# Handing rows to the experts through a table of token numbers, and a rearranged opening, in a two-layer transformer block

## The chip, the cores and the metric

The kernel runs on one core of one Trainium2 chip, in float32 throughout. The metric is the device time of one run in microseconds (us). All data start and end in DRAM (HBM).

## The reference, cut to what matters

The input is `[8, 256, 512]`: 2048 tokens of 512 channels. Two layers follow each other. Each normalises its input and adds attention and a feed-forward network to it, side by side:

```python
xn = layernorm(x)
x  = x + linear_attention(xn)    # 32 heads of 128, decayed in blocks of 32; rms norm, sigmoid gate, output weights
       + experts(xn)
xn = layernorm(x)
x  = x + attention(xn)           # one head of 128, softmax, with biases
       + low_rank_ffn(xn)        # 64 pairs of rank 16, the best 16 of each token

def experts(xt):
    scores = softmax(xt @ router_w + router_b) + router_bias        # 16 experts
    g      = scores in 4 groups of 4; keep the 2 groups with the best maximum
    idx    = the best 2 experts in the groups kept;  gate = their scores, 0 elsewhere
    y      = sum over the experts e of gate[:, e] * ((silu(xt@w1[e]+b1[e]) * (xt@w2[e]+b2[e])) @ w3[e] + b3[e])
    z      = (silu(xt@sw1+sb1) * (xt@sw2+sb2)) @ sw3 + sb3          # shared expert, 256 wide
    return y + z
```

So each token uses two of sixteen experts. `b3` (in the kernel an array of 17 rows) holds the sixteen last biases `b3[e]` and, as row 16, the shared expert's `sb3`.

## The kernel before, in words

**Four chunks.** The tokens are cut into four chunks of 512 (`i` = 0 to 3), each with four tiles of 128 rows.

**The opening** runs the chunks one after the other. `begin` normalises a chunk (`normalize`: statistics, L231 and L232; a square root on ScalarE, L223; scaling, L236) and writes it into `xns[i]`. TensorE turns it, channels onto partitions (`turn_rows`, L243), and VectorE and ScalarE copy it to `xT[i]` (L246, L248). GpSimd makes sums of `xT` that the big products need later (`token_sums`, stored to `xc`). `shared_up` projects the chunk to the shared expert's width (wide products of 512 columns, L312). `route` computes the sixteen router scores by narrow products of 16 columns (L271), and a chain on VectorE ranks them (`first_two`: each score is compared with every other) into the gates `ge` and the choice `sel_all`. `decays` makes the attention's decay tables (stored to `dec`), and `clear` writes zeros from SBUF over a quarter of `xd`, an array in DRAM of 47 tiles of 128 rows. One chunk later `share` calls `shared_down`: it turns the gates (L333), copies them to `geT` (L335), and sums in one bank the product of gates and last biases (L338) and those of the shared expert (L340). The sum is added to `x` (L97 through the helper `tt`) and stored to `xr`.

**The slots.** When all chunks are routed, three products count the tokens of each expert (L482 to L484) and a chain on VectorE gives every pair of token and expert a slot. The slots of one expert begin on a tile of 128, so each of the 47 tiles of slots has one expert. The working tiles of this computation lie in `disp`, which takes the memory of the later accumulator `acc` (pool accp). The tiles of the routing (`sel_all`, `ge`, `before`) lie in the opening's pool, whose memory the next pool, `attn`, takes over; its first tiles `c` are written at L1010 and L1012.

**Attention, 32 units.** A unit is a chunk and a group of four heads; it needs the projections q, k, gate and v for its tokens. These are a large matrix product, made as a scheme of seven block products, `p1` to `p7`, each with weights `w` and tokens `xt` that are sums of blocks (`product`, L666). `ORDER` is the order in which their weights are made. In the first chunk (i = 0) the weights' sums are made on the way: VectorE adds blocks of a loaded tile `st` (`outer_sum`), GpSimd makes further sums, and they are stored to `ws` for the other chunks. For i = 1 to 3 each of the seven is again made by seven products (`p1` ... `p7` of `Outer`). After every group of four products `slot()` is called: it runs the pieces of other work that `later(n, f)` has entered for n slots ahead. The attention's scores, the output product (`project`, L858, whose operands `gT` GpSimd adds), and the experts come in that way. VectorE adds the results (`c`, `r`), GpSimd as well.

**Rows to the experts.** During i = 0 two rows tiles per unit are loaded from `xnd` (`row`), and each is written twice into `xd` by a DMA with computed addresses (`scatter`), 256 KB each, at its tokens' slots:

```python
out=xd[:, :],
out_offset=bass.IndirectOffsetOnAxis(ap=slots[:, n, t : t + 1], axis=0), in_=x_,
```

**Experts.** From unit 8 on, two or three slot tiles are worked per unit, 47 in all. `Expert` loads its tile of `xd` on SP's queue (L696) and gathers its expert's weights from GpSimd (L697). At slot 8 `turn` turns the rows, at 11 `up` computes the hidden values, at 14 `down` multiplies by the last weights, ScalarE copies the result to `ye` (L733) and it goes to `yd`. These tiles come from a ring of two staging buffers (`staged`), which `st`, `spare` and others share.

**Ends of the chunks.** In the last unit of a chunk, `load_sum` loads `xr[i]` into a staging buffer (`spare8`), and `finish` (L592) adds the attention to it; the result goes to `xs_[i]`. For the last chunk this is done in layer 1 (`next_x`). `gather` and `settle` fetch a token's two expert rows from `yd` and add them with their gates. For chunk 0 this stands in the last units (`wrapped_up`), followed by the normalisation for layer 1.

**Layer 1** goes chunk by chunk: `Head` makes the router's narrow products (`route`, 64 columns, L1316), q and k (`qk`, L1310), values, softmax and gates; `low_rank` and the last product use the scheme of seven again (L1434, L1512).

**Who orders the work.** The order in the program text is the order on each engine, save where the tile framework's scheduler moves instructions; in the pool `attn` ScalarE and GpSimd keep the program's order (`manual_schedule`). SP issues the plain DMAs; GpSimd issues those with computed addresses, between its other instructions.

Of the kernel before, what the change touches and what calls it, by code (L numbers as in the profile page):

```python
# [9 lines left out]
FP = mybir.dt.float32  # L10
I32 = mybir.dt.int32
# [55 lines left out]
def block_kernel(  # L67
# [75 lines left out]
    def once(shape, name):  # L143
        return work.tile(shape, FP, tag=name, name=name, bufs=1)

    scratch = big("scratch").rearrange("p (h b) n -> p h (b n)", h=4)
    xs = [work.tile([P, TPC, C], FP, tag="x", name=f"x{i}", bufs=NCH) for i in range(NCH)]
    x_t = x.rearrange("(i t p) c -> i t p c", t=TPC, p=P)
    for t in range(TPC):
        nc.sync.dma_start(out=xs[0][:, t, :], in_=x_t[0, t])  # L150
# [14 lines left out]
    b3_t = held[0 : E + 1, SH * C : (SH + 1) * C]  # L165
    nc.sync.dma_start(out=b3_t, in_=b3)
# [8 lines left out]
    xd = dram.tile([NSLOT, C], FP, name="xd")  # L175
# [7 lines left out]
    xnd = [dram.tile([P, TPC, C], FP, name=f"xnd{i}") for i in range(NCH)]  # L183
# [5 lines left out]
    zero = held[:, (SH + 1) * C : (SH + 2) * C].unsqueeze(1)  # L189
    nc.gpsimd.memset(zero, 0.0)  # L190

    ident = const.tile([P, P], FP, name="ident")
    make_identity(nc, ident)
    eps_t = const.tile([P, 1], FP, name="eps_t")
    nc.gpsimd.memset(eps_t, EPS)
# [5 lines left out]
    before = once([P, E, E], "before")  # L201
# [8 lines left out]
    dist = const.tile([P, S + P], FP, name="dist")  # L210
# [15 lines left out]
    def normalize(o, xc):  # L226

        mv = small.tile([P, TPC, 2], FP, tag="mv", name="mv")
        for t in range(TPC):
            st = small.tile([P, 6], FP, tag="st", name="st")  # L230
            nc.vector.bn_stats(st, xc[:, t, :])  # L231
            nc.vector.bn_aggr(mv[:, t, :], st)  # L232
        rstd = small.tile([P, TPC], FP, tag="rstd", name="rstd")
        rsqrt(rstd, mv[:, :, 1])
        for t in range(TPC):
            nc.vector.tensor_scalar(  # L236
                o[:, t, :], xc[:, t, :], mv[:, t, 0:1], rstd[:, t : t + 1], ALU.subtract, ALU.mult
            )
# [26 lines left out]
    def route(xT, ge, sel):  # L265

        full = [P, TPC, E]
        pl = ps_sc()
        for t in range(TPC):
            for c in range(NC):  # L270
                mm(  # L271
                    pl[:, bass.ts(t, E)], xT[:, c, bass.ts(t, P)], rw[:, c, :],
                    start=(c == 0), stop=(c == NC - 1),
                )
# [31 lines left out]
        tt(ge[:, :, 0:E], sc, sel, ALU.mult)  # L306
        nc.vector.memset(ge[:, :, E : E + 1], 1.0)
# [9 lines left out]
    def shared_up(i):  # L317
        hT = scratch[:, 2 + i % 2, :].rearrange("p (e n) -> p e n", e=SH)
        for e in range(SH):
            p1, p2 = ps_mm(), ps_mm()  # L320
            project(p1, wsh, e, i)
            project(p2, wsh, SH + e, i)
            h1 = work.tile([P, CH], FP, tag="h1", name="h1")
            b1, b2 = bsh_t[:, 0, e : e + 1], bsh_t[:, 1, e : e + 1]
            nc.scalar.activation(h1, p1, AF.Silu, bias=b1)
            nc.vector.scalar_tensor_tensor(hT[:, e, :], p2, b2, h1, ALU.add, ALU.mult)
        return hT

    def shared_down(i, hT):
        xc = xs[i]  # L330
        pg = ps_sc()
        for t in range(TPC):
            nc.tensor.transpose(pg[0 : E + 1, bass.ts(t, P)], gates[i][:, t, :], ident)  # L333
        gT = work.tile([E + 1, CH], FP, tag="geT", name="geT", bufs=1)
        nc.scalar.copy(gT, pg[0 : E + 1, :])  # L335
        for t in range(TPC):
            py = ps_mm()
            mm(py, gT[:, bass.ts(t, P)], b3_t, start=True, stop=False)  # L338
            for e in range(SH):
                mm(py, hT[:, e, bass.ts(t, P)], w3sh[:, e, :], start=False, stop=(e == SH - 1))  # L340
# [4 lines left out]
    sel_all = once([P, NTT, E], "sel_all")  # L345

    def share(i, hT):
        shared_down(i, hT)
        nc.sync.dma_start(out=xr[i], in_=xs[i])
# [60 lines left out]
    def clear(i):  # L410
        lo, hi = (0, 12, 24, 36, NMT)[i : i + 2]
        nc.sync.dma_start(
            out=xd[lo * P : hi * P, :].rearrange("(j p) c -> p j c", p=P),
            in_=zero.to_broadcast([P, hi - lo, C]),
        )

    def begin(i):
        xns.append(work.tile([P, TPC, C], FP, tag="xn", name=f"xn{i}"))
        normalize(xns[i], xs[i])
# [3 lines left out]
    for i in range(NCH):  # L423
# [3 lines left out]
        nc.sync.dma_start(out=xnd[i], in_=xns[i])  # L427
# [8 lines left out]
        ups.append(shared_up(i))  # L436
        ge = once([P, TPC, E + 1], f"ge{i}")
        route(xT[i], ge, sel_all[:, bass.ts(i, TPC), :])
        gates.append(ge)
        decays(i)  # L440
        clear(i)
# [8 lines left out]
    disp = Parts(accp.tile([P, 7 * CH], FP, tag="acc", name="disp"))  # L450
# [50 lines left out]
    nc.vector.tensor_reduce(own, owner, AX.X, ALU.add)  # L501
    nc.vector.tensor_scalar(own, own, float(E - 1), float(P), ALU.min, ALU.mult)
# [14 lines left out]
    for n in range(TOP):  # L517
        tt(hit, slot, ends_[:, n, :].unsqueeze(2).to_broadcast(full), ALU.is_equal)
        tt(hit, hit, sel_all, ALU.mult)
        for i in range(NCH):  # L520
            at_i = bass.ts(i, TPC)
            tt(hit[:, at_i, :], hit[:, at_i, :], gates[i][:, :, 0:E], ALU.mult)
# [63 lines left out]
    def finish(i, r):  # L586

        for b in range(2):
            for t in range(2):
# [4 lines left out]
                )  # L594

# [3 lines left out]
    with tc.tile_pool(name="attn", bufs=1) as attn, tc.manual_schedule(engines={mybir.EngineType.Activation, mybir.EngineType.Pool}):  # L599
# [79 lines left out]
        def slot():  # L679
# [3 lines left out]
            while pieces and pieces[0][0] <= now[0] and n < (2 if len(pieces) > 12 else 1):  # L683
                f = pieces.pop(0)[2]
                f()
                n += getattr(f, "func", f).__name__ not in ("silu", "gate", "row", "scatter", "load_sum", "sums1", "sums2", "sums3", "sums4", "settle0", "settle1", "out_sum")


        class Expert:


            def __init__(self, j):
# [3 lines left out]
                nc.sync.dma_start(out=self.xe, in_=xd[bass.ts(j, P), :])  # L696
# [6 lines left out]
            def turn(self):  # L703
# [4 lines left out]
                nc.vector.tensor_copy(self.xeT, pt.rearrange("p (c n) -> p c n", c=NC))  # L708

# [16 lines left out]
            def down(self):  # L726
# [6 lines left out]
                nc.scalar.copy(ye, py)  # L733
# [888 lines left out]
```

## Time and profile before

| | |
|---|---|
| runs of the kernel before | 2862.28, 2861.57, 2854.19 us; median 2861.57 |
| the profiled execution | 2856.16 us, of which the span in the trace is 2854.4 |
| TensorE products (PE) / weight loads (PEld) | busy 2796.7 / 2566.1 us (98% / 90% of the span) |
| VectorE (DVE), ScalarE (ACT), GpSimd (POOL) | busy 1569.7, 948.2, 1465.7 us (55%, 33%, 51%) |
| DMA | 763.21 MB, mean 267 GB/s |
| granted clock of TensorE | 0.993 |

| stage | from, to (us) | PE busy | 
|---|---|---|
| opening, to the third weight tile (p6) of the first unit | 0 to 186.7 | 160.65 |
| the rest of the first chunk, i = 0 | 186.7 to 764 | 570.31 |
| chunks 1 to 3, with the experts | 764 to 2535 | 1756.48 |
| layer 1 | 2535 to 2854 | 309.22 |

Busy times of the engines overlap, so they don't add up to the span. The stages' limits are read from the timeline, where a stage's first product of TensorE starts. In rows of the trace a tile's name stands for all its buffers, `a<-b` means that `a` is written from `b`, and L with a number is the line of the kernel (L97 is the helper that makes additions, so such rows are told apart by their tiles). A number in brackets at the end of a timeline row is the wait ahead of that group and what ended it.

### The profile page before, as it was taken

What the parts mean: (1) busy time and instruction counts of PE and PEld (TensorE: products, weight loads), DVE (VectorE), ACT (ScalarE), POOL (GpSimd) and SP (SyncE); (2) the same over time, 40 slices, a digit from 0 to 9 for tenths busy, and PEclk for the clock granted to TensorE, in tenths of its full rate; (3) what the DMA queues carried; (4) which work ended last, traced back from release to release, by engine and by line L of the source; (5) the groups of instructions that cost most, each with busy time, mean ns of one, the idle gap of its engine ahead of it and who ended that gap; (6) DMA issues with size and microseconds to landing.
All of it is one profiled execution on the core that took longest, in us unless ns stands there. A gap on an engine that the chain in (4) does not pass through costs nothing. (4 is left out here: it accounts for less than half of the span.)

```text
span 2854.4 us, 49572 instructions
## 1 busy us (share of the span) xinstructions
PE 2796.7 (98%) x19864; PEld 2566.1 (90%) x19864; DVE 1569.7 (55%) x2615; ACT 948.2 (33%) x1683; POOL 1465.7 (51%) x1213
## 2 busy tenths in 40 slices
PE   8989999999999999999999999999999999999999
PEld 4469999999999999999999999999999999987877
DVE  6555666666654445444545555555555555556663
ACT  3312222212244333333443333443444333432221
POOL 4545666665546555555645454545544566552210
PEclk9999999999999999999999999999999999999999
DMA  7888998899986777778877777777777788652211
GB/s 255 301 309 337 357 352 341 341 349 347 364 320 246 262 266 273 282 270 299 296 265 257 264 266 265 259 274 280 284 259 259 267 310 298 222 212 88 76 61 61
DMA packets 161943, 763.21 MB, mean 267 GB/s; under 512 B 18209, under 2 KB 24225, under 8 KB 109874
## 3 DMA queue, kind: packets, MB, share of 16 engines
q1 hardware_dynamic: 149826, 706.25, 66.9%
q0 software_dynamic: 11888, 53.79, 5.2%
q8 instruction: 157, 2.57, 0.4%
q14 instruction: 72, 0.59, 0.1%
HBM read 596.14 MB, written 163.05 MB: 266 GB/s over the span
## 5 line engine op out<-in xcount | busy, mean ns | idle before, releaser
L666 PE MATMUL ps_a<-xt,w 128*128 128x128 f32 x5376 | 750.9, 276 | 11.7 <-DVE r L97 7.7
L666 PEld LDWEIGHTS ps_a<-xt,w 128*128 128x128 f32 x5376 | 681.9, 192 | 30.1 <-issue 14.3
L97 POOL TENSOR_TENSOR c<-c 128x512 f32<-128x512 f32 x216 | 271.7, 1273 | 262.0 <-DVE c L97 259.9
L97 POOL TENSOR_TENSOR c<-c,r 128x512 f32<-128x512 f32 x240 | 318.4, 1347 | 158.9 <-DVE r L97 153.1
L666 PE MATMUL ps_e<-xt,w 128*128 128x128 f32 x2688 | 373.4, 275 | 1.3 <-DVE c L97 1.3
L97 POOL TENSOR_TENSOR sums<-sums,sq 128x512 f32<-128x512 f32 x120 | 153.3, 1278 | 426.4 <-ACT sq L796 425.6
L996 ACT COPY cp<-ps_a 128x512 f32<-128x512 f32 x336 | 196.4, 585 | 476.0 <-PE ps_a L666 468.8
L666 PEld LDWEIGHTS ps_e<-xt,w 128*128 128x128 f32 x2688 | 344.4, 192 | 11.2 <-issue 3.8
L97 POOL TENSOR_TENSOR w<-w 128x512 f32<-128x512 f32 x224 | 294.6, 1325 | 108.2 <-issue 31.2
L666 PE MATMUL ps_a<-w,xt 128*128 128x128 f32 x1792 | 346.7, 275 | 0.0
L858 PE MATMUL ps_sc<-wo,gT 128*128 128x256 f32 x1288 | 305.1, 379 | 1.8 <-POOL gT L97 1.8
L97 DVE TENSOR_TENSOR acc<-ps_sc,acc 128x512 f32<-128x512 f32 x208 | 143.3, 690 | 265.8 <-PE ps_sc L858 198.8
L666 PEld LDWEIGHTS ps_a<-w,xt 128*128 128x128 f32 x1792 | 272.3, 192 | 0.0
L97 DVE TENSOR_TENSOR c<-ps_a,c 128x512 f32<-128x512 f32 x232 | 157.9, 686 | 202.7 <-PE ps_a L666 201.7
L858 PEld LDWEIGHTS ps_sc<-wo,gT 128*128 128x128 f32 x1288 | 232.3, 190 | 26.8 <-POOL gT L97 2.0
L666 PE MATMUL ps_b<-xt,w 128*128 128x128 f32 x1680 | 236.4, 277 | 6.8 <-ACT c L1010 4.2
L801 DVE SCALAR_TENSOR_TENSOR gT<-ps_o,nw,c 128x256 f32<-128x256 f32 x256 | 112.0, 479 | 231.0 <-ACT sq L796 222.0
L666 PEld LDWEIGHTS ps_b<-xt,w 128*128 128x128 f32 x1680 | 217.3, 194 | 17.5 <-issue 8.2
L744 ACT ACTIVATE c<-c 128x512 f32<-128x512 f32 x256 | 148.9, 627 | 170.1 <-DVE c L97 170.0
L796 ACT ACTIVATE sq<-ps_o 128x512 f32<-128x512 f32 x120 | 71.6, 597 | 382.3 <-PE ps_o L782 382.3
L666 PE MATMUL ps_e<-w,xt 128*128 128x128 f32 x896 | 173.2, 275 | 0.0
L97 DVE TENSOR_TENSOR s<-ps_sc,decay 128x384 f32<-128x384 f32 x256 | 139.8, 552 | 40.7 <-PE ps_sc L770 38.1
(299 smaller groups left out, 4635.8 us busy)
## 6 DMA issues: line engine op xcount, KB each, us to landing
w<-in_w_att_dram SPq DMA_DIRECT2D x128, 1024.0 KB
st<-in_w_att_dram SPq DMA_DIRECT2D x32, 1024.0 KB
wo<-in_w_out_dram SPq DMA_DIRECT2D x113, 256.0 KB
decay<-dec SPq DMA_DIRECT2D x64, 384.0 KB
w<-ws0p SPq DMA_DIRECT2D x12, 1792.0 KB
w<-ws1p SPq DMA_DIRECT2D x12, 1792.0 KB
w<-ws2p SPq DMA_DIRECT2D x12, 1792.0 KB
w<-ws3p SPq DMA_DIRECT2D x12, 1792.0 KB
```

What stands on the lines that cost most here:

```text
L97: (eng or nc.vector).tensor_tensor(o, a, b, op)
L666: mm(bank[:, bass.ts(ty, P)], a, b, start=(first and ty == 0), stop=True, skip_group_check=True,)
L744: nc.scalar.activation(qk, qk, AF.Silu)
L796: nc.scalar.activation(sq, po, AF.Square)
L801: nc.vector.scalar_tensor_tensor(gT[:, h, :].rearrange("p (t n) -> p t n", t=2), po[:, bass.ts(h, S)].rearrange("p (t n) -> p t n", t=2), ...
L858: mm(py[:, bass.ts(t, S)], self.O[p][:, hh, bass.ts(t, P)], self.wo[p][:, hh, :], start=(t == 0 and hh == 0), stop=(hh == 1), skip_group_c ...
L996: nc.scalar.copy(c, bank)
```

## The change

The text of the computation is the same; what moves is this.

1. **A table in place of copied rows.** `xd`, its clearing and the loading of rows are gone. An array `table` of one integer per slot is zeroed once; in i = 0 each `scatter` writes 128 token numbers (from `token`, an iota) into it. At the end of i = 0 `read_table` loads the table and `turn_table` turns it by one transpose into `whose`, a tile of 128 x 47 integers. An expert then gathers its rows from `xnd` (now one array of 2048 rows) through `whose`, on GpSimd's queue.
2. **Last biases.** `shared_down` has no gates and no products with `b3`. Each `Expert` gathers its expert's bias into the buffer of its rows once they are turned (`bias`, through `own_`), and VectorE adds it in place of ScalarE's copy to `ye`. `sb3` is added to the rows of `xr` by GpSimd, at `load_sum` or `next_x` (`last_bias`). The slots of an expert's pieces move from 8, 11, 14 to 10, 12, 13, 18.
3. **Opening.** x of chunk 0 comes on two queues and is normalised tile by tile (`apart`); ScalarE's first square root is on a constant. Sixteen transposes of the identity stand at the beginning (`idle`). The router's narrow products stand among the wide ones (`between` in `shared_up`), the next chunk is turned ahead of `share`. `sel_all`, `before` and `ge` lie in `disp`, whose tile is taken first.
4. **Layer 1.** The normalisation in `wrapped_up` is spread over slots; the router products of the first `Head` stand among those of q and k (`opening`).

```diff
+WARM = 8
...
+    disp = Parts(accp.tile([P, 7 * CH], FP, tag="acc", name="disp"))
...
-        nc.sync.dma_start(out=xs[0][:, t, :], in_=x_t[0, t])
+        (nc.scalar if t % 2 else nc.sync).dma_start(out=xs[0][:, t, :], in_=x_t[0, t])
...
-    b3_t = held[0 : E + 1, SH * C : (SH + 1) * C]
-    nc.sync.dma_start(out=b3_t, in_=b3)
...
-    zero = held[:, (SH + 1) * C : (SH + 2) * C].unsqueeze(1)
-    nc.gpsimd.memset(zero, 0.0)
-
+    table = dram.tile([NSLOT, 1], I32, name="table")
+    none = once([NMT, P], "none", I32)
+    nc.gpsimd.memset(none, 0)
+    nc.sync.dma_start(out=table.rearrange("(j p) o -> j (p o)", p=P), in_=none)
+
+    eps_t = const.tile([P, 1], FP, name="eps_t")
+    nc.vector.memset(eps_t, EPS)
+    root = small.tile([P, TPC], FP, tag="rstd", name="root")
+    nc.scalar.activation(root[:, 0:1], eps_t, AF.Sqrt)
...
+    for _ in range(2):
+        idle = ps_o()
+        for n in range(WARM):
+            nc.tensor.transpose(idle[:, bass.ts(n % 4, P)], ident, ident)
...
-    before = once([P, E, E], "before")
+    before = disp.tile([P, E, E], FP, name="before")
...
-        tt(ge[:, :, 0:E], sc, sel, ALU.mult)
-        nc.vector.memset(ge[:, :, E : E + 1], 1.0)
+        tt(ge, sc, sel, ALU.mult)
...
-    def shared_up(i):
+    def shared_up(i, between):
...
             project(p1, wsh, e, i)
+            between()
             project(p2, wsh, SH + e, i)
+            between()
...
-        pg = ps_sc()
-        for t in range(TPC):
-            nc.tensor.transpose(pg[0 : E + 1, bass.ts(t, P)], gates[i][:, t, :], ident)
-        gT = work.tile([E + 1, CH], FP, tag="geT", name="geT", bufs=1)
-        nc.scalar.copy(gT, pg[0 : E + 1, :])
         for t in range(TPC):
             py = ps_mm()
-            mm(py, gT[:, bass.ts(t, P)], b3_t, start=True, stop=False)
             for e in range(SH):
-                mm(py, hT[:, e, bass.ts(t, P)], w3sh[:, e, :], start=False, stop=(e == SH - 1))
+                mm(py, hT[:, e, bass.ts(t, P)], w3sh[:, e, :], start=(e == 0), stop=(e == SH - 1))
...
-        normalize(xns[i], xs[i])
+        normalize(xns[i], xs[i], apart=(i == 0))
...
-        ups.append(shared_up(i))
-        ge = once([P, TPC, E + 1], f"ge{i}")
-        route(xT[i], ge, sel_all[:, bass.ts(i, TPC), :])
+        pl, tiles = ps_sc(), list(range(TPC))
+        ups.append(shared_up(i, lambda: scores(pl, xT[i], tiles.pop(0))))
+        ge = disp.tile([P, TPC, E], FP, name=f"ge{i}")
+        route(pl, ge, sel_all[:, bass.ts(i, TPC), :])
         gates.append(ge)
+        if i + 1 < NCH:
+            turn(i + 1)
         decays(i)
-        clear(i)
...
+    nc.vector.tensor_scalar(own_, own, float(E - 1), None, ALU.min)
...
+    def last_bias(r, t3):
+
+        nc.sync.dma_start(out=t3, in_=b3[E : E + 1].to_broadcast([P, C]))
+        for t in range(TPC):
+            add(r[:, t, :], r[:, t, :], t3, nc.gpsimd)
...
-                nc.sync.dma_start(out=self.xe, in_=xd[bass.ts(j, P), :])
+                nc.gpsimd.indirect_dma_start(
+                    out=self.xe, out_offset=None, in_=xnd[:, :],
+                    in_offset=bass.IndirectOffsetOnAxis(ap=whose[:, j : j + 1], axis=0),
+                    bounds_check=NT - 1, oob_is_err=False,
+                )
...
+            def bias(self):
+
+                nc.gpsimd.indirect_dma_start(
+                    out=self.xe, out_offset=None, in_=b3[:, :],
+                    in_offset=bass.IndirectOffsetOnAxis(ap=own_[:, self.j : self.j + 1], axis=0),
+                    bounds_check=E, oob_is_err=False,
+                )
...
-                nc.scalar.copy(ye, py)
+                add(ye, py, self.xe)
...
-            later(8, e.turn)
-            later(11, e.up)
-            later(14, e.down)
-
-        def row(t):
-
-            x_ = attn.tile([P, C], FP, tag="sum", name="row", bufs=3)
-            nc.sync.dma_start(out=x_, in_=xnd[t // TPC][:, t % TPC, :])
-            for n in range(TOP):
-                later(6 + 10 * n, partial(scatter, x_, t, n))
...
+            later(10, e.turn)
+            later(12, e.bias)
+            later(13, e.up)
+            later(18, e.down)
+
+        def scatter(t, n):
...
-                out=xd[:, :],
+                out=table[:, :],
                 out_offset=bass.IndirectOffsetOnAxis(ap=slots[:, n, t : t + 1], axis=0),
-                in_=x_, in_offset=None, bounds_check=NSLOT - 1, oob_is_err=False,
+                in_=token[:, t : t + 1], in_offset=None, bounds_check=NSLOT - 1, oob_is_err=False,
...
+            rows = attn.tile([P, P], I32, tag="h1", name="rows")
+            nc.sync.dma_start(out=rows[0:NMT], in_=table.rearrange("(j p) o -> j (p o)", p=P))
...
+                nc.vector.tensor_copy(byno[0:NMT], rows[0:NMT])
+                pt = ps_sc()
+                nc.tensor.transpose(pt[:, 0:NMT], byno[0:NMT, :], ident[0:NMT, 0:NMT])
+                nc.vector.tensor_copy(whose, pt[:, 0:NMT])
...
-                normalize(y, x_)
...
+            for t in range(TPC):
+                later(35 + 2 * t, partial(stats, t))
+                later(45 + 2 * t, partial(scaled, t))
+            later(43, whole.root)
...
+        def opening(self):
+
+            self.pf = ps_sc()
+            self.q = work.tile([P, CH], FP, tag="q", name="q1", bufs=1)
+            self.k = work.tile([P, CH], FP, tag="k", name="k1", bufs=1)
+            for n, o in enumerate((self.q, self.k)):
+                pm = ps_sc()
                 for c in range(NC):
...
+                    mm(pm, wqkv_t[:, c, bass.ts(n, P)], self.yT[:, c, :], start=(c == 0), stop=(c == NC - 1))
+                    if c % 2:
+                        self.ranks(2 * n + c // 2)
...
-    head.route()
-    head.qk()
+    head.opening()
```

## The prediction

> **What bounds the kernel now.** I read the page's first two parts, then the busy time by stages, TensorE's waits, and its timeline over the first 187 us.
>
> ```profile
> PE 2796.7 (98%) x19864; PEld 2566.1 (90%) x19864; DVE 1569.7 (55%) x2615; ACT 948.2 (33%) x1683; POOL 1465.7 (51%) x1213
> ...
> PE   8989999999999999999999999999999999999999
> PEld 4469999999999999999999999999999999987877
> ```
>
> TensorE is the bound. Weight loads (PEld) stay at 9 in the long middle, but at 4, 4, 6 in the first three slices of 71 us: there TensorE is occupied with little to show. By stages (busy us of PE, PEld, DVE, ACT, POOL, then clock, DMA share, GB/s):
>
> ```profile
> 0.00:186.70 186.70, 160.65 (x567) 89.67 (x567) 112.73 (x243) 57.25 (x86) 81.94 (x129) 0.94 0.75 276
> 186.70:764.00 577.30, 570.31 (x4412) 550.26 (x4413) 356.45 (x550) 125.02 (x216) 352.31 (x277) 1.00 0.91 348
> 764.00:2535.00 1771.00, 1756.48 (x13399) 1673.54 (x13398) 912.98 (x1386) 705.02 (x1261) 965.36 (x754) 1.00 0.75 273
> ```
>
> The opening (to the third weight tile, p6, at 186.70) has 26 us without TensorE work and a clock of 0.94. The other stages lose 7 and 15 us, so little can be won there. TensorE's waits and its timeline (start, us, name, wait before it):
>
> ```profile
> PE ps_b L666 <- ACT c L1010: 4.2, 1, 4.2
> PE ps_sc L333 <- DVE ge L97: 3.6, 1, 3.6
> PE ps_b L666 <- DVE mv L232: 2.6, 1, 2.6
> ```
> ```profile
> 39.62 3.60 PE L271 MATMUL ps_sc<-rw,xT 128*128 128x16 f32 x16
> 43.05 5.34 PE L312 MATMUL ps_b<-xT,wsh 128*128 128x512 f32 x8
> 48.23 3.60 PE L312 MATMUL ps_a<-xT,wsh 128*128 128x512 f32 x8
> ...
> 97.62 0.60 PE L333 MATMUL ps_sc<-ident,ge 128*17 128x128 f32 x4
> 98.88 1.12 PE L338 MATMUL ps_b<-held,geT 17*128 17x512 f32 x2 [0.66 <-ACT geT L335]
> 99.93 1.98 PE L340 MATMUL ps_b<-held,scratch 128*128 128x512 f32 x4
> 101.85 1.12 PE L338 MATMUL ps_a<-held,geT 17*128 17x512 f32 x2
> ...
> 175.97 1.55 PE L666 MATMUL ps_b<-xt,w 128*128 128x128 f32 x6 [4.20 <-ACT c L1010]
> ...
> 186.70 0.91 PE L666 MATMUL ps_a<-xt,w 128*128 128x128 f32 x6 [1.68 <-DVE w L97]
> ```
>
> Router products (L271, 16 columns) took 3.60 us at 39.62, against 1.85 at 95.92; the wide group after them took 5.34, the next 3.60: the clock had dropped. At 97.62 to 101.85 stands what the expert biases cost per chunk: turned gates, a wait, four products L338 (1.05 from start to start).
>
> [...] a wide record took 0.43 us (3.44 from group to group, eight in a group); the group of 5.34 lost 1.75, as four records at half speed would, 3.5 us long. [...] I give the sixteen idle transposes nothing. [...] the 128x1024 product of the ranking took 2.17 us beside GpSimd's adds at 46.38, 1.22 at 140.43. [...] Measured landings are longer:
>
> ```profile
> xw<-in_w_exp_dram,rows__1106 POOLq DMA_INDIRECT x47, 7.5
> xd<-row,slots POOLq DMA_INDIRECT x32, 7.3
> spare<-yd,slots POOLq DMA_INDIRECT x32, 6.2
> ```
>
> **Opening, worked in time.** Undisturbed pieces: turning a chunk 4 x 0.44 = 1.75; wide 32 x 0.43 = 13.8; narrow 32 x 0.116 = 3.7; shared down 16 x 0.48 = 7.7.
>
> Chunk 0 ended at 35.2. Its rows now come on SP's queue and ACT's, are normalised tile by tile, and ACT's square-root table (1.28 us, at 7.68) is loaded ahead, so turning starts at some 6 instead of 10.2; eight of the idle transposes stand in front of it, eight after its first product (under 2 us). But VectorE's new order puts two statistics of x1 ahead of the copies of xT0, and x1 landed at 13.98; narrow products then begin near 15 (13.66 before), and the clock will have dropped again. I take 35.2 unchanged, bounds -4 (x1 lands earlier, since wsh alone is ahead of it) and +2.
>
> Chunk 1: 1.75 + 13.8 + 3.7 + 1 for the copies: 55.4 (59.3 before; the two dips above cost 1.75 each). Chunks 2 and 3 each with the preceding chunk's shared down between turning and projecting, which covers the copies: 26.9 each, to 82.3 and 109.2 (97.6 and 130.7). That drops 2 x (0.44 + 0.66 + 4.2) = 10.6 of bias work, and dips and waits of turning. Shared down of 2 and 3, 15.4: 124.6 (164.4: bias work again 11, wait 3.6, the cold stretch after it). Then p1 (7.1) with the slot counts (1.9) among it. They need VectorE's ranking of chunk 3: 17.0 after the narrow products (130.83 to 147.84), plus four more adds of x, 2.4: 128.6, so TensorE waits 1.5 and p1 ends at 135.
>
> The 4.20 goes: c shares memory with the opening's pool, and ACT's L1010 waited until VectorE had read the last routing tile at 175.3; these tiles now lie in disp (accp). What is late next is p6's weights: from 130, VectorE has the slot chain (10.1, from 165.05 to 175.14), four c adds (2.6), eight outer sums (5.0): p6 at some 147. Against 186.7 that is **-40**, bounds -25 and -47: GpSimd's contention on VectorE's chain one way, an earlier chunk 0 the other. The freed transfers, four clears of xd of 12.3 MB, are 31 us of DMA at the 396 GB/s of 90 to 100 us, off a stage at share 0.75 of 187: what is left, some 109 us of full DMA, fits into 147, and so I cost the denser writes of xc, dec and xr at nothing; if that cover is gone, a wait of p6 for its st tile takes the place.
>
> **First token group (to 764).** 16 row loads (4.2 MB) and 32 scatters of 256 KB become 32 scatters of 128 words. GpSimd's issue stays 1.0 us each; it no longer waits 19.4 for rows. DMA share was 0.91, TensorE lost 7 us: -1, bounds -4 and +2. Zeroing the table, reading it and turning it are two small DMAs on SP's queue and one product, at its end.
>
> **Experts (47).** TensorE's products are unchanged. xe's load leaves SP's queue (47 issues fewer, beside 16 rows and 4 clears) for GpSimd's, with a bias gather added: 2 x 1.01 us more of GpSimd each, 95 us in a stage where it is busy 965 of 1771. Behind them wait its c and gT adds. ye is added by VectorE (0.69) instead of copied by ACT (0.58). xe has ten slots to land, a slot being 73.1/49 = 1.49 us, so 14.9. The bias has six: issued at slot 12, behind TensorE's turning at 10 (its buffer), used after down at 18, 8.9 us for a landing of 3.8 to 8.9. VectorE being late by some 6 us cost TensorE 2.6 (at 2440), so about 3 us are free. In the first expert unit spare8 takes a staging buffer between experts 0 and 1, so expert 1's gather (slot 17) holds GpSimd until expert 0's down (slot 19): some 3 us, once. I take +3 in all, bounds 0 and +19 (0.4 each).
>
> **Shared bias (last_bias).** Three times in units: four GpSimd adds of 1.27, 5.1 us, behind a load of 1 MB (landing in 3.8 to 8.9) and one of 256 KB on SP's queue, ahead of the gT sums that feed L858 seven slots later (10 us). +3, bounds 0 and +15. In the last chunk, finish waits for them: 3.2 us later on VectorE, where ps_e already waits 1.8 for cp; the spread gates give part back: +2, bounds +1 and +5.
>
> **Late pieces.** Chunk 0's second normalisation, one run of 9.3 us on VectorE at 2436, is spread over slots. It cost the 2.6 wait and, by the cold groups after it (2.05 and 2.31 for 0.89 and 1.79), 1.7 more: -4, bounds -4 and 0. Head 0's ranks among q and k: 14.0 us now, 10.4 at full clock, but ranking starts 6 us later: 0, bounds -3 and +5.
>
> **Sum:** -40 - 1 + 3 + 3 + 2 - 4 = -37; less 1 for unseen waits, -36. The profiled execution took 2856.16 (span 2854.4 plus 1.8), 5.4 below the median 2861.57; taken from the median: **2825**.
>
> **Rivals.**
> 1. Half the opening is kept by another engine. VectorE is busy 113 of 187 us; at the contended 2.17 for 1.22 its chain would set 3 chunks of four by some 6 us each: gain 20 there, 2845. For it: VectorE runs in program order, with the statistics of x2 and x3 ahead of xn1. Against: up to 130 us its windows of before sum to 79, which fits into 109.
> 2. Slower: the bias gather lands late and holds VectorE, which in turn holds TensorE's banks. It decides the whole from 36/47 = 0.77 us an expert on top of the 0.06 taken: with 3 us free, a landing plus GpSimd's own delay of 8.9 + 3 + 0.8 = 12.7. Medians of 6.2 to 7.5 speak against; the longest, 13.0, for. At 1.2 each: 2880.
> 3. The interleaving does not do what it says: dips stay, since four narrow products stand together and ten ahead in chunk 0: 3.6 at chunks 1 and 2 each come back: 2832.
>
> **Chances.** Forecast 0.62 (2811 to 2836), rival 3 0.12, rival 1 0.18, rival 2 0.05, middle between 1 and 2 near zero 0.03. A measurement here tells about 0.3%, 8.6 us. Range 2806 to 2846.
>
> **To check in the profile after.** the first product of p6 near 147; no products like L338; wide groups at 3.60 after narrow ones; ACT's first c copy not waiting on disp; xw gathers' landing under 9; waits of TensorE on VectorE's r and c still under 0.5 each. I am wrong if p6 comes after 165, or if the stage of experts is longer than 1771 by over 10.

## The result, and the profile after

The changed kernel took 2961.66 us (median of 4 runs, 2952.38 to 2965.14), against 2861.58 of the kernel before: ratio 1.0351, interval 1.0321 to 1.0381. It is slower by 100 us where 2825 had been predicted. The profiled execution took 2963.79 us, its span 2962.1.

The page's first parts again, busy time and the 40 slices (74 us each), with the throughput of the DMA:

```profile
PE 2797.9 (94%) x19833; PEld 2580.9 (87%) x19833; DVE 1603.8 (54%) x2665; ACT 919.8 (31%) x1634; POOL 1577.0 (53%) x1323
...
PE   7978888887999999999999999999999999999999
...
DMA  6799999888788777777787777778777778653211
GB/s 247 283 246 259 268 268 267 247 270 255 288 339 299 283 275 273 271 270 269 298 310 267 264 265 266 265 269 307 285 267 267 287 290 312 247 188 131 73 59 59
```

TensorE's hole is no longer in the opening but in slices 3 to 10. There the DMA is busy at 8 or 9 and moves 246 to 270 GB/s; the kernel before moved 309 to 357 in those slices. Later the two rows are alike. By stages (busy us of PE, PEld, DVE, ACT, POOL, clock, DMA share, GB/s; cut at the first product of p6 and at the first and last product `project`, L903 here and L858 before):

```profile
0.00:150.86 150.86, 130.84 (x535) 80.91 (x535) 114.41 (x241) 52.19 (x82) 84.89 (x130) 0.94 0.72 268
150.86:914.50 763.64, 654.74 (x4820) 624.85 (x4821) 371.91 (x599) 145.76 (x251) 369.20 (x296) 0.94 0.90 270
914.50:2602.20 1687.70, 1666.02 (x12697) 1586.17 (x12696) 905.81 (x1355) 644.67 (x1151) 1025.75 (x820) 1.00 0.76 278
2602.20:2962.00 359.80, 346.31 (x1786) 288.96 (x1784) 211.65 (x473) 77.16 (x150) 97.16 (x78) 0.99 0.28 100
```

| stage, us | before | after | difference |
|---|---|---|---|
| opening, to p6 | 186.7 | 150.9 | -35.8 |
| p6 to the first product of chunk 1's `project` | 632.4 | 763.6 | +131.2 |
| to the last of them (experts) | 1678.5 | 1687.7 | +9.2 |
| to the end | 356.8 | 359.9 | +3.1 |

All the damage is in the first token group, whose prediction was -1. TensorE's waits there (total, times, longest):

```profile
PE ps_sc L923 <- DVE gT L846: 45.5, 8, 14.9
PE ps_b L699 <- DMA w<-in_w_att_dram: 35.4, 6, 10.8
```

The second row names weights that come late; VectorE, which the first names, itself waits for weights: in the whole run 102.6 us in 18 waits for `w` and 42.8 for `st`, against 9.6 and 11.8 before. So the DMA sets the pace of this stage, with fewer bytes than before (763.6 us at 270 GB/s against 632.4 at 347). What slows it is seen in windows of 3 us around one scatter of 128 token numbers. GpSimd issues it here:

```profile
310.57 1.00 POOL L1135 DMA_INDIRECT table<-token,slots  x1 [0.15 <-issue]
```

and these are the windows (the last two columns are DMA share and GB/s; the trace records a DMA as packets, and a packet's time and bytes are counted in the window in which it begins):

```profile
309.00:312.00 3.00, 3.00 (x27) 2.95 (x26) 1.27 (x2) 0.00 (x0) 2.75 (x4) 1.00 0.90 374
312.00:315.00 3.00, 3.00 (x25) 2.90 (x24) 1.49 (x4) 0.60 (x1) 3.00 (x3) 1.00 2.22 161
315.00:318.00 3.00, 3.00 (x27) 2.95 (x26) 1.00 (x2) 1.63 (x3) 0.31 (x1) 1.00 0.33 16
318.00:321.00 3.00, 3.00 (x22) 2.79 (x21) 0.62 (x1) 2.31 (x4) 0.00 (x0) 1.00 0.62 60
321.00:324.00 3.00, 3.00 (x21) 2.77 (x20) 0.77 (x2) 0.14 (x2) 0.00 (x0) 1.00 0.76 300
324.00:327.00 3.00, 3.00 (x25) 2.91 (x24) 0.27 (x1) 1.08 (x3) 1.27 (x1) 1.00 1.00 415
```

Some 5 us after the issue hardly a packet of the whole core begins (6 from 315 to 318 us, 16 GB/s), and some 10 us after it the rate is back. I call such a stretch a hold. A share above 1 (2.22) means packets that began in that window and took long: 8 of SP's queue took over 5 us. The trace's record of every packet shows it too: the longest packet of SP's queue, 8 KB, began at 313.9 us and took 8.1 us; in the kernel before no packet of that queue took over 3.0 us. The scatter's own packets, 16 of 32 bytes, are recorded with 15 ns at the median. A dip like this follows the scatters issued at 331.07, 347.44 and 402.87. All but one of the 32 scatters lie in the stage; 131 us over 32 is 4.1 us each. Such a DMA of 512 bytes landed after 11.2 us at the median, while those of 256 KB in the kernel before took 7.3.

### The profile page after: what moved, and what is told of

Its sections match the earlier page's. It is cut to its first block, busy times and chain, and to the rows that moved or that the text cites. A ratio compares the mean times of both kernels' runs of the same rounds, so it can differ in the third digit from the quotient of the medians.

```text
span 2962.1 us, 49662 instructions
## 1 busy us (share of the span) xinstructions
PE 2797.9 (94%) x19833; PEld 2580.9 (87%) x19833; DVE 1603.8 (54%) x2665; ACT 919.8 (31%) x1634; POOL 1577.0 (53%) x1323
## 4 chain that ended last, share of the span: by engine, by line
PE 76%; DMA 11%; DVE 7%; issue 3%; POOL 2%; SPq 1%; ACT 0%; DVEq 0%; POOLq 0%; ACTq 0%
PE ps_a L699 21%; PE ps_e L699 11%; PE ps_sc L903 9%; PE ps_b L699 6%; DMA w<-in_w_att_dram 5%; PE ps_o L826 3%; PE ps_sc L923 3%; PE ps_sc L814 3%; PE ps_sc L761 3%; DMA st<-in_w_att_dram 2%; PE ps_o L827 2%; PE ps_a L1601 2%; PE ps_sc L815 2%; DVE r L98 1%; PE ps_sc L773 1%
## 5 line engine op out<-in xcount | busy, mean ns | idle before, releaser
L903 PE MATMUL ps_sc<-wo,gT 128*128 128x256 f32 x1288 | 304.8, 379 | 1.1 <-POOL gT L98 1.1
L903 PEld LDWEIGHTS ps_sc<-wo,gT 128*128 128x128 f32 x1288 | 232.4, 190 | 26.2 <-POOL gT L98 1.3
L923 PE MATMUL ps_sc<-wo,gT 128*128 128x256 f32 x576 | 148.4, 405 | 47.7 <-DVE gT L846 45.5
```

The lines of the kernel that those rows point to most:

```text
L903: mm(py[:, bass.ts(t, S)], self.O[p][:, hh, bass.ts(t, P)], self.wo[p][:, hh, :], start=(t == 0 and hh == 0), stop=(hh == 1), skip_group_c ...
L923: mm(py[:, bass.ts(h, S)], gT[:, hh, bass.ts(t, P)], self.wo[pair, h][:, hh, :], start=(h == 0 and hh == 0), stop=(hh == 1), skip_group_ch ...
```

## The experiments

Four theories of why the scatters, or something beside them, slow the DMA: A, any write of 4 bytes is dear; B, writes that lie side by side hold each other; C, the arrays in DRAM have moved; D, DMAs with computed addresses disturb.

**1. No scatters.** `scatter` returns at once, and the table is filled once: `nc.gpsimd.iota(none, pattern=[[1, P]], base=0, channel_multiplier=41)`.

> The 32 scatters of token numbers are left out; the table is filled once with fixed, valid token numbers, so the experts work on other rows than they should. Everything else, the arrays' places in DRAM too, is as in the changed kernel. Theory A (each scatter's 4-byte writes hold up the DMA of the whole core for some us): the first token group loses its 131 us, 2962 - 131 = 2831 us, and its DMA moves about 347 GB/s again instead of 270. Theory B (the 4-byte writes are slow because many of them fall side by side, into the same stretch of DRAM): the same, 2831. Rival C (the arrays in DRAM have moved by the 12.3 MB of xd, and loads and stores of weights now disturb each other): no change, 2962. Rival D (a DMA with computed addresses is what disturbs, whatever it writes): 2831.

Measured: 2836.58 us, ratio 0.9918 (0.9892 to 0.9945). `project` began at 787.4 instead of 914.5. With the same arrays at the same places, C falls. One window over most of the first token group, 200 to 640 us, in the changed kernel and without scatters:

```profile
200.00:640.00 440.00, 366.21 (x2643) 348.61 (x2642) 204.64 (x326) 75.94 (x132) 215.11 (x173) 0.92 0.94 264
200.00:640.00 440.00, 438.13 (x3396) 423.08 (x3395) 274.94 (x423) 95.18 (x164) 246.26 (x190) 1.00 0.86 327
```

TensorE is busy 438 of 440 us instead of 366, and no packet of SP's queue took over 2.4 us.

**2. Wide rows.** A slot of the table has 512 bytes, and all of them are written.

```diff
-    table = dram.tile([NSLOT, 1], I32, name="table")
+    table = dram.tile([NSLOT, P], I32, name="table")
...
-                in_=token[:, t : t + 1], in_offset=None, bounds_check=NSLOT - 1, oob_is_err=False,
+                in_=own_row, in_offset=None, bounds_check=NSLOT - 1, oob_is_err=False,
```

> Each slot of the table is 512 bytes wide, and a scatter writes 128 rows of 512 bytes (the token number repeated 128 times, 64 KB) in place of 128 numbers of 4 bytes. Theory A (small writes): the holds go, about 2835 us. Theory B (neighbours): they go too, about 2835. Rival D (computed addresses): unchanged, about 2960.

**3. Far apart.** The same table, but 4 bytes are written in each slot (`apart_` is the slot's number times 128).

> The scatter writes 4 bytes as in the changed kernel, but the numbers of two slots lie 512 bytes apart in DRAM instead of 4. Theory A (a write of 4 bytes is dear by itself): unchanged, about 2960 us. Theory B (writes that fall side by side into one stretch of DRAM wait for each other): the holds go, about 2835. Rival D: unchanged.

Measured: 2881.52 us for the wide rows (1.0088, 1.0062 to 1.0114) and 2880.57 for the numbers far apart (1.0082, 1.0055 to 1.0108). Both lie between the theories, but the profile decides: from 200 to 640 us they move 329 and 324 GB/s, TensorE is busy 435 us, and no packet of SP's queue took over 2.8 and 2.4 us, so there are no holds. The far-apart kernel:

```profile
200.00:640.00 440.00, 434.61 (x3357) 418.97 (x3356) 266.82 (x415) 93.19 (x161) 272.05 (x215) 1.00 0.86 324
```

The 40 us are lost in another place. VectorE waited 29.9 us for the table to be read back into `rows` (its copy of them is `byno`), which with slots 512 bytes apart is 6016 (47 x 128) numbers of 4 bytes, each by itself in DRAM, and in that time hardly anything else came in (1 GB/s from 680 to 700 us); SP's next loads, four of `wo`, stood behind this DMA in its queue. From the far-apart kernel, VectorE's wait, and windows as above:

```profile
DVE byno L1155 <- DMA rows<-table: 29.9, 1, 29.9
```
```profile
640.00:660.00 20.00, 20.00 (x171) 19.69 (x170) 10.70 (x18) 6.63 (x12) 12.37 (x11) 1.00 0.94 346
660.00:680.00 20.00, 13.35 (x98) 12.54 (x96) 7.18 (x10) 4.65 (x8) 5.72 (x5) 0.93 0.37 124
680.00:700.00 20.00, 0.00 (x0) 0.00 (x0) 0.00 (x0) 0.00 (x0) 0.00 (x0) 0.50 0.10 1
```

The kernel with far-apart numbers writes as many pieces of 4 bytes by as many DMAs with computed addresses as the changed kernel. A and D fall; B stands.

**4. Plain small writes.** `nc.sync.dma_start(out=table[at : at + P, :], in_=token[:, t : t + 1])` in place of each scatter.

> In place of each scatter a plain DMA from SP's queue writes the same 128 numbers of 4 bytes from 128 partitions side by side into the table, in the order of tokens and not of slots, so the experts work on other rows. Theories A and B: the holds stay, about 2960 us. Rival D (computed addresses, GpSimd's queue): they go, about 2831.

Measured: 2926.75 us (1.0236, 1.019 to 1.0283), from two runs. From 200 to 640 us:

```profile
200.00:640.00 440.00, 386.13 (x2797) 369.90 (x2798) 213.09 (x343) 75.62 (x131) 198.49 (x155) 0.94 0.97 266
```

Holds stay without computed addresses and without GpSimd, at (2926.75 - 2836.58) / 32 = 2.8 us each. They are shorter than those of the changed kernel, for which the same sum gives (2961.66 - 2836.58) / 32 = 3.9. Why 128 numbers in one stretch of 512 bytes cost less than numbers at scattered slots stays open.

**5. The distance.** The same idea with a table of floats whose slots lie 64, 32, 16, 8 or 4 bytes apart; it is read back in 47 long rows and VectorE picks the numbers out. Beside them 8 bytes with the number in the second half.

```diff
+    nc.vector.tensor_scalar(apart_, ends_, float(16), None, ALU.mult)
...
+            rows = staged("rows")[0:NMT, 0 : 16 * P]
+            nc.sync.dma_start(out=rows, in_=table.rearrange("(j n) o -> j (o n)", n=16 * P))
```

> The numbers of two slots lie 64 bytes apart in the table, and the table is read back whole, in 47 rows of 8 KB, and thinned out on VectorE, so that no read of single numbers is left. Theory B (writes that fall side by side into one stretch of DRAM wait for each other), if the stretch is 64 bytes or less: about 2838 us, as without the scatters (2837). If the stretch is longer (up to the 512 bytes tried): holds stay in part, between 2850 and 2950. Theory A (a 4-byte write is dear wherever it goes): 2960.

> As the kernel whose table has 64 bytes for a slot, with 32 bytes. Theory B: if the stretch in which writes wait for each other is 64 bytes, two slots share one and holds come back in part, between 2870 and 2930 us; if it is 32 bytes or less, about 2853, a little under the 2856 of 64 bytes, since the table that is read back is half as long.

> As the table with 32 bytes for a slot, with 16. If the stretch is 32 bytes, two slots share one: DMA throughput of the first token group falls again and the time lies between 2860 and 2920 us. If the cost falls evenly with distance: about 2865. If the stretch is 16 bytes or less: 2850, as with 32 bytes.

> As the table with 16 bytes for a slot, with 8. If the stretch is 32 bytes, four slots share one: more than with 16, 2890 to 2950 us. If it is 16 bytes, two share one and the first loss shows here, 2860 to 2920; if it is 8 bytes or less, 2850.

> As the table with 8 bytes for a slot, with the number in the second 4 bytes of each slot, so that every address is 4 more than a multiple of 8. If neighbours in one stretch are the cause: the same as with the first 4 bytes, 2855 us, landing near 7.5. If what is dear is a write of 4 bytes at an address that is no multiple of 8 (half of the writes of the changed kernel): holds come back, 2950 or more.

> The end of this series: 4 bytes for a slot, as in the changed kernel, but with the float table and the reading of the others. If the distance of the writes is the cause: holds as in the changed kernel, about 2960 us less nothing for the reading, landing near 11. If something else of these variants (floats, the way the table is read) took the holds away: about 2850.

In the table, landing is the time from the issue of a scatter to its end, and the last column is the longest packet of SP's queue in the profiled execution.

| bytes apart | time, us | ratio, interval | landing, median us | 200 to 640 us: PE busy, DMA share, GB/s | longest packet, us |
|---|---|---|---|---|---|
| 64 | 2856.39 | 0.9986, 0.9977 to 0.9995 | 5.4 | 434, 0.85, 323 | 2.3 |
| 32 | 2850.01 | 0.9969, 0.9959 to 0.9979 | 6.4 | 434, 0.86, 323 | 2.5 |
| 16 | 2847.17 | 0.9956, 0.9943 to 0.9969 | 7.1 | 433, 0.87, 322 | 2.9 |
| 8 | 2855.59 | 0.9989, 0.9976 to 1.0002 | 7.5 | 426, 0.93, 320 | 3.5 |
| 8, second half | 2855.64 | 0.9989, 0.997 to 1.0008 | 8.7 | 426, 0.93, 317 | 4.4 |
| 4 | 2958.65 | 1.0356, 1.0263 to 1.0449 | 11.7 | 368, 0.93, 262 | 7.2 |

With 4 bytes the variant is as slow as the changed kernel, so floats and the other way of reading had no part in the cure. The odd address gives the same time as the even one, though its landing (8.7 for 7.5) and its longest packet are a little longer. There is no step at 32 or 64 bytes, as I had thought there might be: the landing grows with every halving. At 8 bytes there are holds already, but short ones: the share of the DMA rises for the same GB/s (0.93 for 0.87), the longest packet is 3.5 us, and TensorE loses 8 us against 64 bytes. At 4 they are long and TensorE loses 66. In this series the distance, and how many numbers share a stretch of DRAM, change together; which of the two counts is not separated.

The times of 64 to 16 bytes stand above the 2837 without scatters for a good part because of the read back: VectorE waited 16.1, 9.0 and 4.8 us for the rows. That makes 64 slower than 16, whose table is a quarter as long. At 8 bytes this wait is 2.3, and the short holds take its place. With scatters 16 to 512 bytes apart TensorE is also busy some 4 us less than without any (433 to 435 for 438); what takes these 4 us stays open.

**6. The same scatters in the kernel before.**

```diff
                 in_=x_, in_offset=None, bounds_check=NSLOT - 1, oob_is_err=False,
             )
+            nc.gpsimd.indirect_dma_start(
+                out=table[:, :],
+                out_offset=bass.IndirectOffsetOnAxis(ap=slots[:, n, t : t + 1], axis=0),
+                in_=slots[:, n, t : t + 1], in_offset=None, bounds_check=NSLOT - 1, oob_is_err=False,
+            )
```

> The kernel before, with one thing added: each of its 32 scatters of rows is followed by a scatter of 128 numbers of 4 bytes into a table of slots, side by side, that nobody reads. Theory B: the holds come here too, about as many us as scatters without them gave back in the changed kernel (125): 2856 + 125 = 2980. If the damage needs something else of the change: about 2860.

Measured: 2968.02 us (1.0371, 1.0342 to 1.0401); `project` began at 933.6 instead of 819.1, 114.5 later, and the longest packet of SP's queue took 7.9 us. So the damage needs nothing else of the change.

**7. Without a table.** The inverse of the slots is found by TensorE. For each token tile and choice, VectorE marks the row (`count_up` equal to the slot's number modulo 128) and the tile (equal to its quotient, times the token's number), and products add the marks up:

```diff
+                nc.vector.tensor_scalar(
+                    rows_at[:, bass.ts(e, P)], count_up, row_of[:, n, t : t + 1], None, ALU.is_equal
+                )
+                nc.vector.tensor_scalar(
+                    tiles_at[:, e * NMT : (e + 1) * NMT], count_up[:, 0:NMT],
+                    tile_of[:, n, t : t + 1], token[:, t : t + 1], ALU.is_equal, ALU.mult,
+                )
...
+                    mm(
+                        pt[:, 0:NMT], rows_at[:, bass.ts(e, P)], tiles_at[:, e * NMT : (e + 1) * NMT],
+                        start=(e == 0), stop=(e == 3),
+                    )
```

> No table in DRAM: the token of each slot is found by 32 products. For 128 tokens one operand marks the row of their slots in its tile (128 x 128 zeros and ones), the other the tile, with the token's number as the mark (128 x 47); the sum over all tokens is the tile that the experts gather through. Theory B: no holds, 2837 us of the kernel without scatters plus 32 products at about 0.14, so 2841. If something else in the changed kernel's first token group is slow (rival C, moved arrays), it stays above that.

Measured: 2843.6 us (0.9932, 0.9911 to 0.9954); `project` began at 791.5, 4.1 after the kernel without scatters.

**8. The experts' slots.** On top of this, `later(14, e.up)` for 13.

> As the kernel with the products in place of the table, and an expert's up at slot 14 after its turning, not 13. If the six waits of 1.29 us for xeT in the units of three experts come from turn and up standing too close: about 7 us less than that kernel, 2834. If they come from VectorE being late anyhow: the same time.

Measured: 2833.75 us (0.9904, 0.9883 to 0.9925). The stage of the experts went from 1690.6 to 1678.7 us, that of the kernel before (1678.5). TensorE's waits in it before this edit, in the kernel without a table:

```profile
PE ps_a L711 <- DVE r L98: 8.0, 17, 1.6
PE ps_sc L773 <- DVE xeT L757: 7.7, 6, 1.3
PE ps_e L711 <- DVE c L98: 6.1, 2, 4.4
```

and after it:

```profile
PE ps_a L711 <- DVE r L98: 6.9, 17, 0.4
PE ps_e L711 <- DVE c L98: 5.9, 2, 4.2
```

The row of xeT is gone; with it the stage lost 11.9 us in the profiled executions, and the median of the runs 9.9, where 7 had been expected.

**9. The opening's bank.** On the last kernel, ScalarE takes the second projection out of its bank (`nc.scalar.activation(h2, p2, AF.Identity, bias=b2)`), VectorE multiplies later.

> The kernel with the products in place of the table and up at slot 14, with one change in the opening: the second projection of the shared expert leaves its bank by ScalarE (with its bias), not by VectorE, which multiplies later from SBUF. Theory: chunk 2's turning waited 6 to 8 us for a bank because VectorE, in the middle of the ranking of chunk 0, came to this step late; then the wait goes and the third weight tile comes some 5 us earlier, 2829 us. Rival: VectorE's own chain sets the opening's end anyhow, then the wait moves to the copies of xT or the sums of the shared expert, and the time stays at 2834.

Measured: 2840.05 us (0.9928, 0.9903 to 0.9953), about 6 more than the base, which was measured in another series (0.9904, 0.9883 to 0.9925). The wait only changed its name; first the base, then this run:

```profile
64.25 1.12 PE L267 MATMUL ps_a<-ident,xn 128*128 128x128 f32 x4 [6.26 <-DVE scratch L351]
65.74 3.78 PE L361 MATMUL ps_b<-held,scratch 128*128 128x512 f32 x4 [7.92 <-DVE xT L272]
```

The rival holds as to the place: VectorE, in its order, is late with all that TensorE needs at 58 us, and freeing one bank leaves the copies of xT behind the ranking. That the time grew was forecast by neither; the wait is 1.7 us longer, and the rest stays open.

**10. The shared expert's bias.** On the same base, `last_bias` on VectorE.

> The same base, with the last biases of the shared expert (sb3) added on VectorE (four adds of 0.69 us) instead of GpSimd (four of 1.27). If the waits of 4.2 and 1.7 us at the ends of chunks 1 and 2 and of 3.5 in layer 1 come from the sums of acc on GpSimd, which stand behind these adds: some 5 us less than the base, 2829. If the sums on GpSimd are late for other reasons: the same, 2834; if VectorE has no room there: up to 5 more.

Measured: 2825.46 us (0.9883, 0.9858 to 0.9908), the fastest whole kernel of these runs. And without it:

> The same base without the last biases of the shared expert: sb3 is loaded and added nowhere, so this term is left out of the result. It prices last_bias whole: the prediction's terms for it were 3 us in the units and 2 in the last chunk, so 2829 by them; by the waits seen after (4.2 + 1.7 + 3.5 less what stood there before, 3.1) up to 6 us, 2828. The same time as the base would mean that these waits have another cause.

Measured: 2821.73 us (0.9868, 0.9844 to 0.9893). The term cost 12 us on GpSimd by the medians and 10 by the ratios (the base's are of another series), and costs 4 on VectorE. In the profiled executions, taking it out shortened the experts' stage by 3.4 us (1678.7 to 1675.3) and the last by 7.3 (361.6 to 354.3). GpSimd's four adds stood ahead of the seven sums of `acc` (9.4 us together), for which `finish` on VectorE waited 3.4 us (seen at 1391 us in the kernel without scatters), and behind `finish` stood the sum that frees ps_e. With the adds on VectorE the longest wait for c at a chunk's end fell from 4.2 to 1.7 us. In the fastest whole kernel TensorE is busy 2769.8 of 2822.8 us (98%).

## Why the prediction was wrong

**First token group: the step that failed.** The prediction counted 32 scatters of 128 words at their issue (1.0 us on GpSimd) and at their bytes, and wrote -1 with bounds -4 and +2. Measured: +131.2 us; without the scatters +2.6 (152.4 to 787.4 against 632.4). An operation of a new form, 4-byte pieces side by side in DRAM, was priced by the row of another, and its effect on the transfers beside it was not asked for at all; no rival named it. The two signs of being wrong that the prediction listed did not come either (p6 at 150.9 is not after 165, and the experts' stage grew by 9.2, not by over 10): both look past this stage. The profile before had the warning: DMA share 0.91 and TensorE idle only 7 us, so a hold of the DMA there had little slack before it reached TensorE (busy 366 us from 200 to 640 us here, 438 without the scatters). The size of the writes alone was not enough: 4 bytes written 16 to 512 bytes apart left the throughput almost as it was (322 to 324 GB/s against 327); the neighbours made it dear. SP's packets of up to 8.1 us (2.4 without the scatters) show that other transfers were slow beside these writes; no run shows where they waited.

**Opening: right in kind, 4 us too much.** p6 came at 150.86 where 147 was predicted (186.70 before). No products like L338, wide groups at 3.60 to 3.68 after narrow ones (one of 5.92 in chunk 0), c's first copy waiting 0.4. The end of chunk 1 fell almost as worked out (56.1; 55.4 predicted; chunk 0 ended 1.9 late and chunk 1 was 1.2 shorter), that of chunk 2 did not (91.7; 82.3). The term at fault is the turning of chunk 2 without a wait: it waited 8.0 us for a bank that VectorE freed late (L355), after the ranking of chunk 0, whose first two 1024-wide products took 4.52 us together here and 2.77 before. That is rival 1's mechanism in one chunk of four. That only 4 us of the 9 remained is luck: the pieces behind it had been priced too long (chunk 3 took 25.9 us for 26.9, the last shared downs 14.0 for 15.4 since a product took 0.43 and not 0.48, the rest to p6 19.3 for 22.4).

The sixteen idle transposes had been given nothing, which was an assumption of the author's. In this trace they quickened:

```profile
9.96 0.96 PE L271 MATMUL ps_a<-ident,xn 128*128 128x128 f32 x4
10.76 0.60 PE L271 MATMUL ps_e<-ident,xn 128*128 128x128 f32 x4
15.52 4.45 PE L295 MATMUL ps_sc<-rw,xT 128*128 128x16 f32 x20 [3.73 <-DVE xT L276]
```

Nothing but transposes had run, the last of them without a gap since 7.35, and at 10.76 four took 0.60 us, as they do later at a granted clock of 1.00 (0.60 at 56.60). In the kernel before, whose first sixteen ran alone from 10.22 to 13.66, four took 1.06 to 1.08 all along. Then TensorE waited 3.73 us for VectorE's copy of xT, and twenty router products took 4.45 us at a granted clock of 0.50 (from 14.10 to 24.34), where sixteen take 1.86 later at 1.00 (at 38.91). So the transposes' pace was gone when the first products began, and no gain from it shows, as forecast.

**Experts: right in what was feared, wrong in what cost.** The bias gather landed in 4.1 to 6.7 us, far from the 12.7 at which rival 2 decides, though VectorE did wait for it six times, 9.6 us in all. The stage lost 9.2 us where the terms that fall into it (experts +3, shared bias +3, late pieces -4) make +2. Most of it came from slots: the third expert of a unit found VectorE amid a run of c and r sums, six times 1.29 us. "TensorE's products are unchanged" was true, and their places were not.

**Shared bias and end.** In the units +3 and in the last chunk +2 were predicted. Experiment 10 prices them at 3.4 and 7.3, so the units were right in size and the last chunk was not. In the units the way was another than assumed: the adds delay not only `gT` but the sums of `acc`. In the last chunk TensorE waited 4.2 us for `cp` with the adds on GpSimd and not at all without the term (1.8 before); the other 3 us are not traced. The last stage became 3.1 us longer, +2 predicted; the normalisation's wait of 2.6 is gone, as predicted.

**The sum without the scatters**, from that run's profile (p6 at 152.4, `project` from 787.4 to 2476.0, span 2838.0): -34.3 for the opening (predicted -40), +2.6 for the first token group (-1), +10.1 for the experts' stage (+2), +5.2 for the last (+2), so -16.4 where -37 had been summed. The rest of the change makes the kernel faster, as forecast, but by about half: by the medians of that series 19.1 us (2836.58 against 2855.67).

## What to carry to other kernels

A transfer that is small in bytes can be large in time, and for others (512 bytes cost 3.9 us of the kernel's time here): if a stage lives on DMA, look at GB/s in windows of a few us around each new kind of transfer before costing it by its issue. Put scattered numbers apart (16 bytes were enough here), or keep them off DRAM: 32 small products found the same table for 4 us. When pieces move to other slots, ask of each who else uses its engine there.

## What the runs showed of the hardware

- DMAs that wrote 128 numbers of 4 bytes from 128 partitions, side by side in DRAM, held the core's other DMAs. Around one of them the rate fell from 374 to 16 GB/s, and packets of SP's queue took up to 8.1 us (2.4 without these writes). The loss was 3.9 us of the kernel's time per DMA with scattered slots, and 2.8 with one stretch of 512 bytes.
- At 8 bytes apart the holds were short (packets of up to 3.5 us, TensorE lost 8 of 440 us against 64 bytes apart); at 16 and more none could be told (packets of up to 2.9 us).
- One DMA of SP's queue read 6016 numbers of 4 bytes, 512 bytes apart. VectorE waited 29.9 us for it, and hardly anything else came in meanwhile (1 GB/s from 680 to 700 us). SP's next loads stood behind it; whether it would have held another queue is not shown.
- In the changed kernel transposes alone, without a gap from 7.35 us, brought TensorE to the pace that it had later at a granted clock of 1.00: four took 0.60 us at 10.76, and 0.60 at 56.60. In the kernel before, sixteen alone from 10.22 to 13.66 us did not: four took 1.06 to 1.08.
- Why writes side by side hold the other transfers was not found.
